# A fused two-layer graph kernel: new hand-written orders, one queue for half of layer 0's weights, TensorE transposes for the last batch

## The chip, the cores and the metric

The kernel runs on one core of a Trainium2 chip. A core has a matrix engine (TensorE, PE in the profile, with its weight loads listed apart as PEld), three engines that work on rows of 128 partitions (VectorE or DVE, ScalarE or ACT, GpSimd or POOL) and SyncE (SP), which here only issues DMAs. Each engine works through its own queue in order, and engines wait for one another by semaphores. The metric is the device time of one launch in microseconds.

## The reference

There are 64 batches of 256 tokens with 512 features and one weighted adjacency matrix per batch. Two layers follow each other, each with a residual and a layer norm:

```python
# layer 0
deg = jnp.sum(adj, axis=-1, keepdims=True)
agg = jnp.einsum('bij,bjf->bif', adj, x) / jnp.maximum(deg, EPS)
h   = relu(jnp.einsum('bnf,of->bno', jnp.concatenate([x, agg], axis=2), W))
x   = _layernorm(x + h)
# layer 1: 8 heads of 64
q, k, v = proj(Wq, bq), proj(Wk, bk), proj(Wv, bv)
scores = jnp.einsum('bhqd,bhkd->bhqk', q, k) * SCALE
attn = softmax(scores * (adj + adj)[:, None], axis=-1)
ctx = jnp.einsum('bhqk,bhkd->bhqd', attn, v)
x   = _layernorm(x + (jnp.einsum('bse,fe->bsf', ctx, Wo) + bo))
```

Everything is in float32.

## The kernel before, in words

**Steps and orders.** The kernel is a set of small steps, kept by name in a dictionary, and three texts that say in which order they are issued: START for the first batches, PLAN for one turn, which is run 28 times and takes two batches on, and END for the last batches. In START a word is name:batch, in PLAN name+n or name-n (batches counted from the turn's first), in END name:n with n counted back from 64, so that `:1` is the last batch, 63. Nothing reorders the steps afterwards: each engine gets its instructions in the order of the text. A step that uses a result waits for it by semaphore, and everything behind that instruction on the same engine waits as well.

**Products.** All large products are cut into 2 x 2 blocks and done with seven block products in place of eight (a Strassen-Winograd scheme). A letter names the product and a digit the block product: P (the first two batches) and L (later ones, by pairs of batches, cut twice; L546) are x times W of layer 0; Y is adj times the aggregate half (L709); Q makes q and k (L620); V and O are Wv and Wo (L493). The needed sums of blocks are steps of their own, mostly on POOL (xS, Ls, aS, bS, yS, cS; L432 and L567), for weights at the start (W0s, W0i, Wqs, Wvs, Wos). Results come out of PSUM by steps with k or j in the name: Yk and Yj on DVE (L731), Ok and Oj on DVE (L658, L474), Vk and Qk on ACT. Le takes L's results.

**Banks.** PSUM has eight banks, handed out in turn. A Y product group uses two. In the bank Ycb, the sums c (Y5, then Y3 on top) lie in the left half and b (Y2) in the right one: Y5, Yk5, Y3, Yj3 and Y2, Yj2 are the writers and readers of the two halves, and a product into one half waits for the readers of the other that stand before it in the order.

**Layer 0.** A batch's x is loaded twice: by Dx as rows, and by Dzx in blocks from which DVE makes the transposed xT0 and xT1 (L397). Dza and aT do this for adj, Dadj loads adj as rows, and deg is on DVE. After L (or P) and Y come relu and residual (AYr), statistics (AYb), factors on POOL (AYp, L671 to L673) and the norm on ACT (AYn, L677). The result is written to DRAM by Dway (L764) and read again by Dz1 (L770), turned by x1T (L777), and by Drest (L785) as the residual of layer 1, to which the step bo adds the output bias on POOL (L791). There is one buffer for rest.

**Layer 1.** The heads go in four pairs, a to d. For each: scores S (L812, eight products of 64 rows), m (mask and row maximum on DVE, L828), M (negation on POOL, L841), e and f (exponentials on ACT, L847), r (reciprocal of the sum, L859), n (the scaling on ACT, L864). The weights then have to be turned: T (32 x 32 blocks by DVE, L871), Dw (one DMA to DRAM, L876), Ds (four DMAs back, L884). C0a, C0b, C1a and C1b are the context products (L900), c0 and c1 copy them out (L916), O follows with the sums cS, then the norm (lb, lp, ln) and Dout (L939, four DMAs per batch).

**Weights.** They are loaded once in START by SP, except layer 0's W, which comes in two halves of its contraction, W0h0 and W0h1. Each half has two parts, part 0 for x and part 1 for the aggregate, each of four DMAs of 128 KB (L299, called from L301 to L305): part 1 is issued by ACT's queue, part 0 by SP's. The products of the first half's blocks are P1 and P5; from P2 on, the second half is used too. At most eight DMAs are in flight, since each takes one of eight semaphores. bv1 to bv3 fold bv times Wo into bo at the start.

The turn of PLAN has two places with contexts and scores (S, C). Around Y of the second batch it reads:

```
... Y6+3 Mb+1 Ok5+0 ed+1 O7+0 Yk6+3 aS4+3 Yj2+3 Ls51+4 Y3+3 ...
... V7+1 bS4+2 Dsa+0 V2+1 Vj7+1 xS1+4 Yj3+2 Y2+2 ...
```

Of the kernel before, what the change touches and what calls it, by code (L numbers as in the profile page):

```python
# [6 lines left out]

F32 = mybir.dt.float32
AF = mybir.ActivationFunctionType
# [3 lines left out]
P = 128  # L13
# [10 lines left out]
    Dzx:0 W0h0:0 Dzx:1 W0h1:0 xT0:0 xT1:0 Wv:0 xS3:0 xS1:0 P1:0 W0s1:0 xT0:1 P5:0 Dza:0 xT1:1 xS1:1 P1:1  # L24
    xS2:0 Wb:0 P5:1 Pk1:1 Pk1:0 Pk5:1 xS2:1 Dadj:1 Pk5:0 P2:0 W0s2:0 aT:0 Dadj:0 P6:0 W0i5:0 P6:1 W0s3:0
    Pk6:0 xS4:0 Dx:0 aS1:0 W0s4:0 aS3:0 P3:0 Wvs1:0 Pk6:1 Pj2:0 Dzx:2 P7:0 Pj3:0 deg:0 bS1:0 Y5:0 Pj7:0
    Y1:0 bS3:0 P4:0 Yk1:0 Dza:1 bS2:0 aS2:0 Pk4:0 Y6:0 Wq:0 Yk6:0 aS4:0 Yk5:0 xS3:1 Y7:0 xT0:2 Y3:0
    bS4:0 Y2:0 Yj3:0 Wvs2:0 Yj7:0 Yj2:0 Y4:0 AYr0:0 P7:1 xS4:1 AYb0:0 Yk4:0 AYp0:0 P2:1 AYr1:0 AYb1:0
    AYn0:0 xT1:2 P3:1 AYp1:0 Pj7:1 aT:1 AYn1:0 Dzx:3 Pj2:1 aS3:1 aS1:1 Pj3:1 deg:1 bS1:1 Dway:0 bS3:1
    Y5:1 Wo:0 Y1:1 Yk5:1 aS2:1 P4:1 W0i1:0 bS2:1 Yk1:1 Pk4:1 bv1:0 WqS:0 Y2:1 Y6:1 Dz1:0 xT0:3 Yk6:1  # L30
    Ls11:2 xT1:3 Y7:1 aS4:1 xS1:2 Wqs1:0 Y3:1 Dx:1 bv2:0 xS1:3 Yj7:1 Ls51:2 Ls52:2 bS4:1 L11:2 bv3:0
    L55:2 Dza:2 Le11:2 xS3:2 L15:2 Yj3:1 Y4:1 Ls12:2 Ls53:2 L16:2 Ls54:2 x1T:0 L51:2 L12:2 Le51:2 L52:2
    Le16:2 Yj2:1 yS1:0 L56:2 Yk4:1 Q1:0 Wqs2:0 Wvs3:0 AYr0:1 Ls13:2 Q5:0 Qk1:0 Wqs4:0 Le56:2 aT:2 V5:0
    AYr1:1 V1:0 yS2:0 AYb1:1 L17:2 Wvs4:0 Vk1:0 Q6:0 Wqs3:0 Ls14:2 yS3:0 W0i7:0 L57:2 Qk6:0 AYp1:1 V6:0
    AYb0:1 Qk5:0 Q7:0 yS4:0 W0i4:0 Vk6:0 AYp0:1 AYn1:1 V7:0 Le52:2 xS3:3 AYn0:1 Qj7:0 Q3:0 Le55:2 Dway:1
    Vk5:0 Le15:2 Drest:0 V3:0 Q4:0 Vj3:0 Le57:2 Le12:2 Qj3:0 L13:2 Le17:2 Vj7:0 L53:2 L14:2 Le53:2 L54:2
    Le13:2 Le14:2 V4:0 W0i6:0 Dz1:1 Le54:2 xS2:3 Qk4:0 Ls71:2 Sa:0 aS1:2 Vk4:0 W0i3:0 xS2:2 Sb:0 Dzx:5
    Ls61:2 Ls72:2 L61:2 ma:0 Ls63:2 V2:0 L2:2 mb:0 Ma:0 Dadj:2 Ls73:2 ea:0 Ls62:2 Wos1:0 L65:2 Lj2:2
    fa:0 L2:3 Le61:2 Ls64:2 Mb:0 Wos3:0 L66:2 eb:0 Q2:0 Le66:2 Lj2:3 fb:0 Vj2:0 Le65:2 L67:2 ra:0 na:0
    L63:2 Le67:2 L62:2 Qj2:0 L64:2 Le62:2 xS4:2 Sd:0 Le64:2 Le63:2 xS4:3 x1T:1 Sc:0 Ls31:2 L75:2 md:0  # L40
    yS1:1 Dzx:4 L72:2 L31:2 La12:2 L71:2 mc:0 L35:2 V5:1 Md:0 La12:3 ed:0 Q1:1 Le72:2 Dadj:3 Le31:2
    Ls32:2 Le75:2 Ls74:2 Le71:2 Ls33:2 L76:2 Mc:0 L36:2 aS3:2 Dx:2 Le76:2 ec:0 L73:2 Ls34:2 Le36:2 L41:2
    yS3:1 rb:0 Le35:2 fc:0 L77:2 deg:2 L37:2 Ls43:2 Q5:1 fd:0 Ls41:2 Le73:2 Le37:2 La22:2 Ta:0 nb:0 V1:1
    yS2:1 Le77:2 Dwa:0 Le41:2 L33:2 Qk1:1 Ls42:2 rc:0 L74:2 Le33:2 Ls44:2 L46:2 rd:0 Tb:0 bS3:2 nc:0
    L34:2 L32:2 bS1:2 Q6:1 Le32:2 Le74:2 Vk1:1 Le34:2 Qk5:1 La22:3 Tc:0 L45:2 nd:0 L42:2 Le45:2 Dwc:0
    Y5:2 Le46:2 V6:1 Dwb:0 Le42:2 Vk5:1 Dsa:0 L47:2 Vk6:1 yS4:1 L43:2 Qk6:1 Le47:2 Y1:2 bS2:2 Td:0 V3:1
    aS2:2 Wos2:0 Yk1:2 L44:2 Dwd:0 V7:1 Y6:2 Q3:1 Yk6:2 Dsb:0 Le43:2 xT0:5 bS4:2 xT0:4 Y2:2 Q7:1 xT1:5
    Dsc:0 Vj3:1 xS1:5 Vj7:1 Ls11:4 Y7:2 Qj7:1 Wos4:0 Q2:1 xT1:4 Yj7:2 bo:0 Yj2:2 Dsd:0 Y4:2 Yk5:2 Q4:1
    Yk4:2 AYr1:2 Qj2:1 Dza:3 aS4:2 V4:1 Qk4:1 Qj3:1 xS1:4 Le44:2 Y3:2 Ls53:4 Vk4:1 Yj3:2 Sa:1 AYb1:2
    C0a:0 AYr0:2 AYp1:2 C1a:0 AYb0:2 AYn1:2 ma:1 AYp0:2 C1b:0 C0b:0 xS3:5 AYn0:2 deg:3 Ls51:4 Sc:1 c0:0  # L50
    Dway:2 Ls12:4 aT:3 c1:0 Ls14:4 Sb:1 mc:1 aS1:3 bS1:3 Sd:1 mb:1 V2:1 Mc:1 bS3:3 ec:1 Y1:3 cS1:0 Y5:3
    md:1 fc:1 O2:0 bS2:3 O5:0 aS2:3 Yk1:3 Ma:1 Dx:3 aS3:3 L51:4 Ls13:4 Y6:3 Le51:4 Ls52:4 O1:0 ea:1
    Yk6:3 cS3:0 Y2:3 cS2:0 Dz1:2 Ok1:0 L56:4 Vj2:1 aS4:3 Y7:3 Yk5:3 Md:1 rc:1 L15:4 Yj2:3 bS4:3 nc:1
    L12:4 Yj7:3 Y3:3 Mb:1 Y4:3 O6:0 Yk4:3 fb:1 Yj3:3 L11:4 Oj2:0 cS4:0 L2:5 Ok6:0 Le11:4 Ok5:0 eb:1
    Ls54:4 AYr0:3 AYb0:3 fa:1 L16:4 L2:4 AYr1:3 AYp0:3 ed:1 AYb1:3 Le56:4 L55:4 Tc:1 AYn0:3 AYp1:3 O7:0
    fd:1 L52:4 Dwc:1 Oj7:0 L57:4 x1T:2 AYn1:3 Dza:4 O3:0 Le15:4 Le55:4 rb:1 rd:1 L13:4 yS1:2 Le16:4
    Le57:4 nd:1 L53:4 Le13:4 xS3:4 Dway:3 L17:4 O4:0 Le17:4 Ls73:4 ra:1 Oj3:0 L14:4 Td:1 L54:4 Q5:2
    Le54:4 xS2:5 nb:1 Ok4:0 Le12:4 xS2:4 Lj2:4 Ls61:4 lb0:0 V5:2 Le14:4 na:1 lb1:0 Q1:2 lp0:0 Dz1:3
    Lj2:5 Ls71:4 Ta:1 V1:2 Ls62:4 lp1:0 Q2:2 Vk1:2 Le53:4 Qk1:2 Dwa:1 Tb:1 yS2:2 ln1:0 yS3:2 L65:4 Dwb:1
    V6:2 Ls63:4 Dwd:1 Ls64:4 Dsc:1 L61:4 Vk6:2 Q6:2 Vk5:2 Le61:4 ln0:0 Qk5:2 L62:4 yS4:2 Qk6:2 V7:2 Q3:2  # L60
    Dsd:1 L66:4 Q7:2 Le66:4 Dsa:1 Vj7:2 Le65:4 Le62:4 Le52:4 V3:2 L67:4 Vj3:2 V2:2 Qj7:2 Le67:4 V4:2
    Qj3:2 Dsb:1 Vj2:2 L63:4 Qj2:2 Q4:2 Dout:0 L64:4 Qk4:2 Le64:4 Sa:2 Le63:4 Vk4:2 aT:4 La12:4 C1a:1
    x1T:3 Dx:4 C0a:1 xS4:4 xS4:5 ma:2 C0b:1 Ls31:4 yS1:3 C1b:1 Ls72:4 La12:5 Drest:1 c1:1 Sd:2 c0:1
    Dadj:4 Sb:2 md:2 Ls33:4 Ls32:4 Sc:2 Ls34:4 cS1:1 mb:2 L75:4 Md:2 L71:4 Ma:2 O2:1 mc:2 Mb:2 aS1:4
    L72:4 Dzx:7 fb:2 Ls74:4 L35:4 L32:4 aS3:4 Le71:4 ea:2 L31:4 Mc:2 Le35:4 L76:4 bo:1 Le31:4 O5:1 ec:2
    Dadj:5 deg:4 L33:4 eb:2 L36:4 Le75:4 Le76:4 L73:4 fa:2 Le36:4 cS2:1 L77:4 Le72:4 O1:1 Le73:4 Ls41:4
    ed:2 Ok5:1 Ls42:4 rb:2 Le32:4 L37:4 Ls44:4 Ok1:1 nb:2 Y1:4 cS3:1 Le33:4 O6:1 Le77:4 Le37:4 L74:4
    ra:2 cS4:1 Ok6:1 fc:2 V5:3 Tb:2 bS1:4 O7:1 fd:2 yS3:3 Yk1:4 Dwb:2 Oj2:1 O3:1 La22:4 Dzx:6 rc:2 Oj7:1
    nc:2 L34:4 Oj3:1 O4:1 Le74:4 rd:2 Le34:4 La22:5 Q5:3 na:2 Tc:2 Dwc:2 L41:4 nd:2 yS2:3 Y5:4 Le41:4
    Dsb:2 V1:3 Ls43:4 Ok4:1 lb0:1 bS2:4 L45:4 Vk1:3 aS2:4 L46:4 Ta:2 Qk5:3 lp0:1 Q1:3 Vk5:3 Td:2 Dwa:2  # L70
    V6:3 Qk1:3 Le46:4 Dwd:2 Le45:4 L42:4 Dsc:2 ln0:1 L47:4 Y6:4 Le47:4 Vk6:3 Q6:3 lb1:1 aS4:4 bS3:4
    Yk6:4 Y7:4 Dsa:2 Qk6:3 yS4:3 L43:4 V7:3 lp1:1 Le43:4 Le42:4 L44:4 Yk5:4 bS4:4 Q7:3 Yj7:4 ln1:1 xT0:7
    xT1:7 Dout:1 Y3:4 xS1:7 Qj7:3 Y2:4 bS3:5 Y4:4 Yj2:4 V3:3 Vj7:3 Dza:5 Yk4:4 Q4:3 Yj3:4 xT1:6 deg:5
    Q2:3 AYr1:4 Dsd:2 AYr0:4 Q3:3 AYb1:4 Drest:2 Le44:4 AYp1:4 xT0:6 V4:3 Vj3:3 AYb0:4 xS1:6 AYn1:4
    C0a:2 Ls11:6 Qj3:3 Qk4:3 AYp0:4 Qj2:3 C0b:2 Vk4:3 aT:5 C1a:2 AYn0:4 aS1:5 bS1:5 Dway:4 C1b:2 Ls53:6
    c1:2 Ls13:6 Sb:3 aS3:5 c0:2 Ls12:6 Sd:3 mb:3 bo:2 Sa:3 md:3 Sc:3 Y1:5 cS1:2 O2:2 ma:3 Dz1:4 Mb:3
    Y5:5 O5:2 bS2:5 Yk1:5 mc:3 Y2:5 aS2:5 Dx:5 O1:2 cS2:2 Ma:3 Y6:5 Ok5:2 cS3:2 V2:3 Ok1:2 bS4:5 Yk5:5
    Oj2:2 L11:6 aS4:5 Yj2:5 O6:2 Le11:6 Ls51:6 Yk6:5 fb:3 Ls14:6 Y7:5 Ok6:2 Md:3 Y3:5 cS4:2 Yj7:5 eb:3
    O7:2 Yj3:5 Ls52:6 x1T:4 fa:3 Y4:5 L51:6 O3:2 Yk4:5 ea:3 yS1:4 Oj7:2 Vj2:3 L2:7 Mc:3 Le51:6 Ls54:6
    AYr1:5 fd:3 AYb1:5 ed:3 L55:6 rb:3 L16:6 ra:3 AYp1:5 AYr0:5 O4:2 nb:3 AYb0:5 L52:6 xS3:7 Ok4:2 L56:6  # L80
    Oj3:2 AYp0:5 AYn1:5 L15:6 lb0:2 Q1:4 Le56:6 AYn0:5 Le15:6 L57:6 Dway:5 Le16:6 na:3 Dza:6 L17:6 Q5:4
    Le17:6 Tb:3 Le55:6 Qk1:4 L14:6 rd:3 Le57:6 Dwb:3 V5:4 Le52:6 ec:3 L53:6 Dadj:6 L54:6 Le14:6 Vk5:4
    L13:6 Lj2:7 Le54:6 xS2:7 L12:6 fc:3 Le53:6 L2:6 yS2:4 Le13:6 Qk5:4 xS2:6 rc:3 Ta:3 Ls61:6 nc:3 Q6:4
    lp0:2 lb1:2 Dwa:3 Dsb:3 Le12:6 lp1:2 Lj2:6 nd:3 V1:4 Tc:3 Q2:4 Ls62:6 yS3:4 Vk1:4 Td:3 Dwc:3 ln1:2
    Qk6:4 V6:4 Qj2:4 Dwd:3 L61:6 Dsa:3 Vk6:4 yS4:4 Q7:4 ln0:2 Le61:6 xS3:6 Ls63:6 Ls64:6 L65:6 Qj7:4
    Dout:2 Ls73:6 L62:6 L66:6 Le62:6 Q3:4 Le66:6 Le65:6 V3:4 Dsc:3 L67:6 Vj3:4 V7:4 L63:6 Dsd:3 Vj7:4
    Q4:4 deg:6 Le67:6 Qj3:4 V4:4 Qk4:4 L64:6 Vk4:4 Le64:6 xS4:7 Sb:4 Dz1:5 aT:6 xS4:6 Sc:4 Le63:6 Ls31:6
    La12:6 C0a:3 Drest:3 C0b:3 Ls71:6 aS1:6 C1a:3 Dzx:9 mb:4 Ls32:6 La12:7 C1b:3 mc:4 c1:3 Sd:4 Mb:4
    c0:3 Dx:6 Mc:4 Ls72:6
"""  # L90
PLAN = """
# [63 lines left out]
def kernel(  # L155
# [36 lines left out]
    nc = tc.nc  # L192
# [108 lines left out]
    def load_half(h):  # L301
        @step(f"W0h{h}")
        def _(_):
            load_weights(nc.scalar, w0_raw, 1, w0t[F:], slice(2 * h, 2 * h + 2))
            load_weights(nc.sync, w0_raw, 0, w0t[:F], slice(2 * h, 2 * h + 2))  # L305
# [692 lines left out]
```

## Time and profile before

| what | value |
|---|---|
| median of 3 runs | 3033.29 us (3032.24 to 3034.77) |
| the profiled execution | 3032.66 us |
| its span | 3030.7 us |
| instructions | 59847 |
| PE busy, granted clock over the span | 98%, 0.996 |
| DVE, POOL, ACT busy | 73%, 60%, 54% |
| DMA | 513.88 MB, 170 GB/s on average |

The profile is of one execution. It lists busy time by engine, the span in 40 slices, the groups of instructions by line with what they waited for, and the DMAs with the time from issue to landing. "Line" is the line of the kernel's source. Times of the order "start, duration" come from the trace of that execution; the mark in brackets behind an instruction is the idle time before it and what the trace took to be its releaser. Ends of matmuls are modelled, so their busy time overlaps, while their starts are recorded. DMAs issued show as SPq or ACTq, the queue of the engine that issues them.

Some durations that the parts below use: a 128 x 256 ACT exponential 0.50 us and its row sum, the DVE transpose T 1.23, Drest 6.0 from issue to landing, the writes wsa, wsb and wsc to DRAM 2.9 to 3.9.

### The profile page before, as it was taken

Reading aid. Unit: us, or ns where it says so; the run is one execution under the profiler, and the core shown is the slowest. Engines: PE = TensorE matmul, PEld = TensorE weight load, DVE = VectorE, ACT = ScalarE, POOL = GpSimd, SP = SyncE. Lnnn points to the kernel's source line nnn. Section 1 sums busy time; section 2 is a strip of 40 time slices with the busy share of each in tenths; the row PEclk is TensorE's granted clock in tenths of the full one; section 3 lists DMA queues with packets and bytes.
Section 4 is the critical chain, followed back from the end, with each engine's and each line's share of the span. In section 5 each row is a group of like instructions: output and inputs, shape, how many; then the busy total and the mean of one; then the engine's idle time right before and its main releaser. Section 6 shows DMA issues by size and latency. Waiting matters only on the chain.

```text
span 3030.7 us, 59847 instructions
## 1 busy us (share of the span) xinstructions
PE 2975.6 (98%) x18668; PEld 2530.5 (83%) x18668; DVE 2223.1 (73%) x6148; ACT 1628.6 (54%) x4995; POOL 1822.8 (60%) x3313
## 2 busy tenths in 40 slices
PE   7999999999999999999999999999999999999997
PEld 4888888888888888888888888888888888888885
DVE  6877777777777777777777777777777778777774
ACT  2556555455564555554555645655546556456565
POOL 4656656656566566566565666665665656656543
PEclk9999999999999999999999999999999999999998
DMA  7566675776766766657667566666676675676665
GB/s 160 135 190 176 158 186 155 179 184 158 178 166 155 188 173 162 182 154 181 177 163 182 160 161 182 173 166 179 155 183 180 159 185 156 167 181 171 161 178 146
DMA packets 494282, 513.88 MB, mean 170 GB/s; under 512 B 113936, under 2 KB 392464, under 8 KB 493968
## 3 DMA queue, kind: packets, MB, share of 16 engines
q1 hardware_dynamic: 493328, 509.02, 64.9%
q8 instruction: 151, 2.47, 0.4%
q10 hardware_dynamic: 640, 1.05, 0.2%
q14 instruction: 163, 1.34, 0.2%
HBM read 308.55 MB, written 201.33 MB: 168 GB/s over the span
## 4 chain that ended last, share of the span: by engine, by line
PE 94%; DVE 2%; POOL 1%; DMA 1%; issue 1%; SPq 0%; ACT 0%; DVEq 0%; POOLq 0%
PE Qa L620 15%; PE pc L900 7%; PE Qc L620 7%; PE Va L493 7%; PE Oa L493 6%; PE Qb L620 4%; PE Vc L493 4%; PE Oc L493 4%; PE Ya L709 4%; PE Ycb L709 3%; PE L L598 3%; PE scd L812 2%; PE scc L812 2%; PE sca L812 2%; PE scb L812 2%; PE Ob L493 2%
## 5 line engine op out<-in xcount | busy, mean ns | idle before, releaser
L636 ACT ACTIVATE qk<-Qa,bqk 128x128 f32<-128x128 f32 x768 | 218.9, 370 | 289.5 <-PE Qa L620 289.5
L677 ACT ACTIVATE x<-oy,mv 128x512 f32<-128x512 f32 x128 | 103.8, 811 | 337.8 <-POOL mv L673 319.3
L432 POOL TENSOR_TENSOR xS<-xT,xS 128x256 f32<-128x256 f32 x64 | 46.7, 732 | 267.3 <-PE L6a L546 182.9
L671 POOL TENSOR_SCALAR mv<-mv 128x1 f32<-128x1 f32 x256 | 70.2, 274 | 215.3 <-DVE mv L666 172.4
L916 ACT COPY cT<-pc 128x512 f32<-128x512 f32 x128 | 71.7, 587 | 224.2 <-PE pc L900 224.0
L847 ACT ACTIVATE sa<-sa,nmaxa 128x256 f32<-128x256 f32 x256 | 126.8, 498 | 107.9 <-POOL nmaxa L841 71.3
L432 POOL TENSOR_TENSOR yS<-yS,x1T 128x256 f32<-128x256 f32 x64 | 46.6, 728 | 214.0 <-PE Vc L493 208.3
L731 DVE SCALAR_TENSOR_TENSOR oy<-Ya,deg,oy 128x256 f32<-128x256 f32 x256 | 121.9, 476 | 65.0 <-PE Ya L709 61.9
L828 DVE CUSTOM_DVE_ANT_0 sd<-scd,adj 128x256 f32<-128x256 f32 x256 | 93.3, 421 | 98.1 <-PE scd L812 98.0
L847 ACT ACTIVATE sc<-sc,nmaxc 128x256 f32<-128x256 f32 x256 | 127.0, 501 | 64.2 <-POOL nmaxc L841 64.2
L791 POOL TENSOR_TENSOR rest<-rest,bo_sb 128x512 f32<-128x512 f32 x128 | 160.5, 1276 | 0.2 <-issue 0.2
L672 POOL TENSOR_TENSOR mv<-mv,neg_half 128x1 f32<-128x1 f32 x256 | 145.0, 567 | 21.3
L620 PEld LDWEIGHTS Qa<-yS,Wq 128*128 128x128 f32 x1024 | 124.2, 192 | 15.6 <-issue 13.4
L658 DVE TENSOR_TENSOR rest<-Oa,rest 128x256 f32<-128x256 f32 x192 | 81.0, 422 | 76.3 <-PE Oa L493 60.8
L636 ACT ACTIVATE qk<-Qc,bqk 128x128 f32<-128x128 f32 x256 | 73.5, 380 | 110.0 <-PE Qc L620 110.0
L828 DVE CUSTOM_DVE_ANT_0 sc<-scc,adj 128x256 f32<-128x256 f32 x256 | 93.2, 421 | 53.2 <-PE pc L900 53.2
L432 POOL TENSOR_TENSOR cS<-cT 128x256 f32<-128x256 f32 x128 | 93.6, 731 | 63.2 <-ACT cT L916 63.2
L847 ACT ACTIVATE sd<-sd,nmaxd 128x256 f32<-128x256 f32 x256 | 127.2, 501 | 5.8 <-POOL nmaxd L841 5.8
L847 ACT ACTIVATE sb<-sb,nmaxb 128x256 f32<-128x256 f32 x256 | 127.3, 501 | 3.9 <-POOL nmaxb L841 3.9
L432 POOL TENSOR_TENSOR yS<-x1T 128x256 f32<-128x256 f32 x128 | 94.2, 736 | 56.4 <-DVE x1T L777 54.9
L620 PEld LDWEIGHTS Qa<-yS,Wq_sums 128*128 128x128 f32 x1024 | 124.3, 192 | 3.7 <-issue 0.5
L620 PEld LDWEIGHTS Qa<-x1T,Wq 128*128 128x128 f32 x1024 | 124.4, 192 | 3.3
(289 smaller groups left out, 10047.4 us busy)
## 6 DMA issues: line engine op xcount, KB each, us to landing
zx<-in_x_dram SPq DMA_DIRECT2D x256, 128.0 KB, 3.7
x<-in_x_dram SPq DMA_DIRECT2D x256, 128.0 KB, 3.3
way<-x SPq DMA_DIRECT2D x64, 512.0 KB, 3.2
z<-way SPq DMA_DIRECT2D x256, 128.0 KB, 4.0
rest<-way SPq DMA_DIRECT2D x64, 512.0 KB, 6.0
wsa<-sa SPq DMA_DIRECT2D x64, 512.0 KB, 3.9
wsc<-sc SPq DMA_DIRECT2D x64, 512.0 KB, 2.9
wsb<-sb SPq DMA_DIRECT2D x64, 512.0 KB, 3.5
```

Of the source, the lines that this page charges most:

```text
L432: steps[f"{s}{k}"] = lambda b: engine.tensor_tensor(place(b, k == 3), left(b), right(b), op)
L493: nc.tensor.matmul(ps[:, :width].rearrange("p (m o) -> p m o", o=G), lhsT=left(k, b, c), rhs=w(OUTER[k])[:, :, c], start=first and c == 0, ...
L620: nc.tensor.matmul(ps.rearrange("p (m j q) -> p m j q", m=2, j=2)[:, m, j], lhsT=wqk(OUTER[k])[:, m, c, j * P : (j + 1) * P], rhs=left_y(k ...
L636: nc.scalar.activation(part_q(b, t, n)[:, m, j], ps.rearrange("p (m j q) -> p m j q", m=2, j=2)[:, m, j], AF.Identity, bias=bqk[:, m, c : ...
L672: nc.gpsimd.tensor_tensor(mv[:, 1:2], mv[:, 1:2], neg_half, ALU.pow)
L709: nc.tensor.matmul(ps[:, G:] if acc == "b" else ps[:, :G], lhsT=left(b), rhs=right(b), start=k in (5, 1), stop=True, skip_group_check=True,)
L731: nc.vector.scalar_tensor_tensor(h, ps[:, G:] if acc == "b" else ps[:, :G], held["deg", b][:, t : t + 1], h, ALU.mult, ALU.add)
L791: nc.gpsimd.tensor_tensor(rest, rest, bo_sb, ALU.add)
L812: nc.tensor.matmul(sc(b, j)[:, t], lhsT=qk[d, 0, hp, t * P : (t + 1) * P], rhs=qk[d, 1, hp].rearrange("d (t b m) -> d b t m", t=NT, m=L), ...
L828: nc.vector.tensor_tensor_reduce(out=s[:, :, :, r], in0=sc(b, j)[:, t].rearrange("p (a c l) -> p a c l", a=A, l=L), in1=held["adj", b][:, ...
L847: nc.scalar.activation(rows(b)[:, r], rows(b)[:, r], AF.Exp, bias=of("nmax", b)[:, r : r + 1], accum_out=of("total", b)[:, r : r + 1],)
L900: nc.tensor.matmul(ps[j * D : (j + 1) * D, hp % 2], lhsT=held["v", b][:, c, h * D : (h + 1) * D], rhs=held[f"s{name}", b][:, :, c, j * NT ...
```

## The change

Three things change.

1. All three order texts are replaced. The steps are the same ones, apart from point 3. In the new PLAN, Y3 and Y2 of the two batches stand so, and the contexts and scores of one place are grouped (four contexts, then four scores):

```diff
-... Y6+3 Mb+1 Ok5+0 ed+1 O7+0 Yk6+3 aS4+3 Yj2+3 Ls51+4 Y3+3 ...
+... Y6+3 Dza+4 L15+4 Yk6+3 aS4+3 O7+0 cS4+0 rc+1 Ok5+0 nc+1 Yj2+3 Y3+3 ...
-... Y5+3 Dx+3 mc+1 O1+0 Ma+1 cS3+0 fa+1 Y1+3 O5+0 Ok1+0 Dz1+2 mb+1 Y2+3 ...
+... Y5+3 O1+0 aS2+3 Dz1+2 cS2+0 Y1+3 Ok1+0 L51+4 Ls12+4 Yk5+3 Y2+3 ...
-... Drest+1 L63+4 Vk4+2 L64+4 ... Mc+2 c0+1 Mb+2
+... La12+4 C0a+1 c1+1 C0b+1 xS4+4 Ls31+4 Drest+1 c0+1
```

The last pair of lines is the end of the turn; the bias step of the same batch, bo-1 in the next turn, is its 20th word before and its 27th after.

START begins with batch 1 in place of batch 0, and Wo is loaded where Wv was:

```diff
-    Dzx:0 W0h0:0 Dzx:1 W0h1:0 xT0:0 xT1:0 Wv:0 xS3:0 xS1:0 P1:0 W0s1:0 xT0:1 P5:0 Dza:0 xT1:1 xS1:1 P1:1
+    Dzx:1 W0h0:0 Dzx:0 W0h1:0 xT0:1 xT1:1 xS1:1 W0s1:0 P1:1 Dza:0 xT0:0 xT1:0 P5:1 Pk1:1 xS1:0 Wo:0
```

In END, the last batch's scores come as "V4:1 Qj3:1 Q4:1 Vk4:1 Dsd:2 Qk4:1 Sb:1 Sa:1 ...", where before Q4, V3, V4 and V2 of that batch came after its first scores, "Sa:1".

2. Part 1 of W0h1 goes to SP's queue:

```diff
-            load_weights(nc.scalar, w0_raw, 1, w0t[F:], slice(2 * h, 2 * h + 2))
+            load_weights(nc.sync if h else nc.scalar, w0_raw, 1, w0t[F:], slice(2 * h, 2 * h + 2))
```

3. For the last batch, T, Dw and Ds of all four head pairs are gone. n writes its rows to a new tile sn, which takes the place of layer 0 buffers, and the turning is done by TensorE against an identity that POOL makes (step id: a memset and a select), into a PSUM bank, from which ACT (c = 0) and DVE (c = 1) copy to the layout that C reads:

```diff
+            if last(b):
+                size, tag = ((2 * NT * F, "oy0"), (NT * F, "xT0"), (NT * F, "xT1"), (NT * F, "xS"))[hp]
+                tile_of(f"sn{name}", b, [P, size], tag=tag)
...
+        def by_tensor(c):
+            @step(f"X{name}{c}")
+            def _(b):
+                ps = bank(f"X{name}{c}", b)
+                for r in range(R):
+                    k = r * N + c * P
+                    nc.tensor.transpose(ps[:, r * P : (r + 1) * P], of("sn", b)[:, k : k + P], held["ident", b][:, :P])
+
+            @step(f"XC{name}{c}")
+            def _(b):
+                dst = of("s", b)[:, :, c].rearrange("k b r m -> k r b m")
+                src = held[f"X{name}{c}", b].rearrange("k (r b m) -> k r b m", r=R, m=L)
+                if c == 0:
+                    nc.scalar.copy(dst, src)
+                else:
+                    nc.vector.tensor_copy(dst, src)
```

That is 32 TensorE transposes of 128 x 128, four copies on ACT and four on DVE, in place of four DVE transposes, four DMAs out and sixteen DMAs back. In END they come as "Xc1 Xc0 ... Xa0 ... XCc1 ... Xb0 Xb1 XCa0 Xd0 XCb0 Xa1 XCd0 Xd1 XCa1 XCc0 XCb1 Drest C1a XCd1 C0a C0b C1b" of batch 63.

## The prediction

> **What bounds the kernel now.** I read the page's head and clock row first, then busy time by stretches, then the waits of TensorE, then its instructions in order of time around those waits.
>
> ```profile
> span 3030.7 us, 59847 instructions
> PE 2975.6 (98%) x18668; PEld 2530.5 (83%) x18668; DVE 2223.1 (73%) x6148; ACT 1628.6 (54%) x4995; POOL 1822.8 (60%) x3313
> PEclk9999999999999999999999999999999999999998
> ```
>
> The profiled execution took 3032.66 us, 1.96 of them outside its span; the median is 0.63 above it. TensorE (PE) is the bound, at full clock. But its busy time is modelled, so 98% doesn't say what is to be had. I went by the distance from matmul to matmul instead. Back to back a 512-column product takes 0.429 us, a 256-column one 0.216, a 128-column one 0.112 (below: sixteen of Q start 1.78 apart), a score or context matmul 0.108. Priced so, the kernel's products come to 2907.2 us. So 123.5 us are recoverable at most: 33.5 up to 275.0 us (12.8 of them before the first product), 58.7 in the 28 turns (92.76 each, for 90.66 of products: 2.10), 22.2 in the last stretch, and 9.0 behind the last product.
>
> ```profile
> core 0: us, PE busy (x) PEld busy (x) DVE busy (x) ACT busy (x) POOL busy (x), PEclk, DMA share, GB/s
> 0.00:100.00 100.00, 76.33 (x334) 51.16 (x335) 67.87 (x141) 25.17 (x64) 51.83 (x82) 1.00 0.68 148
> 1500.00:2000.00 500.00, 498.12 (x3155) 426.67 (x3154) 370.82 (x1039) 268.99 (x829) 306.58 (x562) 1.00 0.66 170
> 3000.00:3030.70 30.70, 12.59 (x52) 8.75 (x52) 4.52 (x11) 2.80 (x4) 7.36 (x12) 0.67 0.37 98
> ```
>
> The idle time lies at the two ends, and at the end the granted clock is 0.67.
>
> ```profile
> PE Pa L576 <- DMA W<-in_w0t_dram: 12.8, 1, 12.8
> PE pc L900 <- DMA sb<-wsb: 7.9, 1, 7.9
> PE Ycb L709 <- POOL xs L567: 5.5, 28, 0.2
> PE pc L900 <- DMA sa<-wsa: 2.8, 1, 2.8
> ```
>
> Three waits to look at: layer 0's weights at the start, the last batch's attention weights on their way through DRAM, and one that recurs in each of the 28 turns. The last is named after POOL, but the order of time shows another releaser:
>
> ```profile
> 1997.40 1.03 PE L493 MATMUL Oa<-Wo,cS 128*128 128x256 f32 x4
> 1997.60 0.48 DVE L731 SCALAR_TENSOR_TENSOR oy<-Ya,deg,oy 128x256 f32<-128x256 f32 x1
> 1998.00 0.47 DVE L731 SCALAR_TENSOR_TENSOR oy<-Ycb,deg,oy 128x256 f32<-128x256 f32 x1
> 1998.63 0.67 PE L709 MATMUL Ycb<-oy,aS 128*128 128x256 f32 x2 [0.20 <-POOL xs L567]
> ```
>
> Y3 writes one half of the bank Ycb; Yj2 on DVE (1998.00 to 1998.47) reads the other, behind Yk6 (1997.60). The four O7 products (0.86) end their slots at 1998.26, Y3 starts at 1998.63: 0.37 here, 0.44 averaged over the turns. Y2 waits likewise, for Yj3 behind Vj7: 0.38. The rest of a turn's 2.10 us is 1.29 of changes between full, score and context products.
>
> **The turn: -5.6 us (range -9 to 0).** No work is added or taken away; products stay 90.66. I walked the new order.
> - Changes: before, one of the two places goes context, scores, full (0.55), the other scores, context, scores, full (0.75), 1.29. After, both are all contexts, all scores, full: 2 x 0.55 = 1.09. Gain 0.20.
> - Y3+3 now has L15+4 and O7 between Y6 and itself, 0.43 + 0.86 = 1.30. In that time DVE does Yk6 0.39, rc 0.09, Ok5 0.34, Yj2 0.48, in its order; with 0.2 from product to DVE and 0.15 back that is 1.6 to 1.7. It stays about 0.4 late. Queued behind Y3 on PE is everything.
> - Y2+3 has Y1 and L51, 0.43 + 0.43, after O1, but waits for Yk5 behind Ok1 on DVE: 1.1 against 0.86. With the allowance by which the same sum falls short of before's two waits (0.15), 0.38 late. The turn's other products keep 0.15 us or more, and the loads of turned weights (Ds) are issued 4.7 us earlier than the contexts need them, 6.75 before.
> So the waits stay: 0.20 x 28 = 5.6. At worst a margin of 0.15 fails and takes that back; at best one of the waits shrinks by 0.1.
>
> **The start: -5.0 us (range -8 to +1).** The first four of zx, 128 KB each, have landed at 8.2 us; transfers of 128 KB land one per 0.62. Before, part 0 of the first half of W0 (SP's queue) landed at 9.6 to 12.7, interleaved with part 1 of the second half (ACT's queue), which nobody needs before 18 us. After, that second half is behind the first on SP; ACT's queue holds four. The first half is complete near 10.7, so P1:1 starts 2.1 us earlier. P2's weights, the second half, still land near 18.2 (the total is unchanged), and the four DMAs moved stand ahead of za, Wo and adj on SP; at 1.0 us of issuing each (4.12 for four of W0 before) that alone delays these by some 4. From there it is my walk: P7 (1.46 of waiting before), the two Y waits of 1.1 and that of 2.2 lose their causes, since batches are interleaved the other way round; the p_bv wait for Wo (1.97) goes, since Wo takes Wv's early place among the loads. I get Q's first product at 53 to 54.4 against an equal point at 60.4, 6 to 7.4 gained. Against it: Wv comes late (near 58.8; V5 waits 0.9) and DVE is 90% busy from 60 to 100 us. I take 5.0. Below zero: if the transfers of Wq, way and Wv push z1 back by 7, all is lost again; one more us is what the late Wv could cost.
>
> **The end: -2.4 us (range -7 to +2).**
>
> ```profile
> 2975.19 1.13 PE L812 MATMUL sca<-qk 64*128 64x256 f32 x8
> 3006.85 1.98 PE L900 MATMUL pc<-sb,v 128*64 128x256 f32 x8 [7.90 <-DMA sb<-wsb]
> 3008.58 1.86 PE L900 MATMUL pc<-sc,v 128*64 128x256 f32 x8
> 3010.27 1.05 PE L900 MATMUL pc<-sd,v 128*64 128x256 f32 x8
> ```
>
> The last batch's first scores start at 2975.19, the span ends 55.5 later. ACT ends nd at 2997.2; then comes DVE's transpose (1.23), the write to DRAM, the load, and pc starts at 3006.85 at half clock. After, the order puts four more products of Q and V before the first scores (1.78 + 3 x 0.86 = 4.4). From those scores on: ACT has sixteen exponentials (0.49 each), four n (1.6 each), copies and a layer norm in a row and ends nd 22.9 later; Xd (8 x 0.11), its copies from PSUM and the two last contexts take 5.9; c1 0.6, cS1 0.75, bo 2.5, cS2 0.73, the O products, norm and output as now, 17.9 at full clock (19.6 before, partly at 0.67). Sum 46.7, against 55.5 less 4.4: -4.4. Removed are 4 transposes on DVE and 20 DMAs; the 8 copies hang on ACT (behind nd) and DVE, which idles then. The two make_identity instructions on POOL run while POOL is idle.
>
> Clock. A transpose is a 128-column product; the nearest row is Q's:
>
> ```profile
> 63.69 1.95 PE L620 MATMUL Qa<-x1T,Wq 128*128 128x128 f32 x16
> 65.47 1.95 PE L620 MATMUL Qc<-yS,Wq_sums 128*128 128x128 f32 x16
> ```
>
> By it 32 transposes take 3.6 us. The Trainium skill ("TensorE: Matmul & The Clock Gate", Part 4: PE-mode transpose) speaks against the change: about 275 ns each in a kernel, and they don't count as work for the clock. By the page the 32 take 8.8, and 24 of them lie in PE's idle time; d's eight add 1.3. If the clock falls to half before d's contexts, these and the O products behind pay what before paid: (1.70 - 0.86) a context, up to 4 in all. I take 2 of these 4 away from 4.4. At best (-7) ACT's row is 2.5 shorter, at worst everything is at half clock and the copies out of PSUM, whose target lies in pieces of 32, cost double.
>
> **Sum.** 5.6 + 5.0 + 2.4 = 13.0; 3032.66 - 13.0 = 3019.7 for an execution like the profiled one, 3020.3 by the median. I give 3020.
>
> **The rivals.**
> 1. *The turn's two waits vanish.* For: they are the only waits that recur, and the change moves what stands before them. Against: the walk above finds both still 0.3 to 0.4 short. Both gone: 28 x 0.82 = 23 more, 2997; one gone: 3009. Chance 0.13.
> 2. *The start's gain is given back and the end stays cold.* For: bytes are unchanged, the DMA share is 0.68 in the first 100 us; at 100 us it is DVE's queue that leads. Against: P1 demonstrably waits for W0. 3020.3 + 5.0 + 2.4 = 3027.7: no change. Chance 0.13.
> 3. *Slower, by one mechanism: rest comes late in the turn.*
>
> ```profile
> rest<-way SPq DMA_DIRECT2D x64, 512.0 KB, 6.0
> ```
>
> Drest+1 now stands 6.0 us of PE's work before bo-1 (10.8 before), where the row's median is 6.0 us and the slowest 9.2. If rest is late, POOL stands at bo, with Ls34 (slack 1.0 to L34) and cS2 (2.3 to O6) queued behind it; PE then waits at L34. With 0.4 of margin before POOL, it costs from a landing of 7.4 us on, and the whole gain from 13/28 = 0.46 more: about 7.9 in every turn. If the typical landing under the new order is 8.5, 28 x 1.1 = 31 against 13 gained: about 3051. Against: only one in ten lands over 7.7 now, and those would cost some 0.3. Chance 0.08.
>
> The likeliest case holds 0.66, from 3012 to 3027. The range reaches over most of the first two rivals: 3003 to 3029. What can be told from no change is 0.2%, 6.1 us, so faster is below 3027.2: 0.66 and the first rival's 0.13, less a little for the upper end: 0.78. Same: 0.15. Slower, above 3039.4: 0.07.
>
> **What would show it.** In the profile after: 92.55 us per turn, with Ycb still waiting some 0.4 twice (wrong if the waits on L709 shrink or L34 appears among them); the first product near 10.8 and Q's first near 54; no wait for sb<-wsb, nd to the last pc some 6 us, the transposes 0.11 or 0.28 apart and PEclk between 0.5 and 1 in the last 30 us; rest landing in about 6 us with bo not waiting. If bo waits for DMA in most turns, the third rival has it.

## The result, and the profile after

The changed kernel takes 3019.61 us (median of 5 runs, 3019.02 to 3021.61) against 3033.29 for the kernel before: a ratio of 0.9957, with a 95% interval from 0.9943 to 0.9972. Its profiled execution is one of 3019.61 us, with a span of 3017.7, 13.0 us less than before. The head and the clock row of its page:

```profile
span 3017.7 us, 59666 instructions
...
PE 2972.0 (98%) x18700; PEld 2541.1 (84%) x18700; DVE 2219.4 (74%) x6148; ACT 1638.0 (54%) x4999; POOL 1818.5 (60%) x3315
...
PEclk9999999999999999999999999999999999999999
```

The shares of busy time are within a point of those before, so they can't show what changed. What does is the trace, cut at the first product of the first turn and at the first one of END. Products are priced as in the prediction, and stalls are the rest of a stretch:

| stretch | before | after | products before, after | stalls before, after |
|---|---|---|---|---|
| up to the first turn | 275.2 | 268.3 | 241.6, 239.0 | 33.6, 29.3 |
| the 28 turns | 2597.3 | 2593.1 | 2538.6, 2538.6 | 58.7, 54.5 |
| END and what follows | 158.2 | 156.3 | 127.0, 133.2 | 31.2, 23.1 |

The new START holds 2.6 us of products less and END as much more, and 3.6 us of END are the transposes. So the stretches gained 4.3, 4.2 and (8.1 less 3.6) 4.5 us. The first of these is the least certain, since one execution is compared with one: in the six profiled executions with the old START the first turn began at 273.8 to 278.8 us, half of them below 275, and in the three with the new START and queue at 268.3 to 268.5. The waits of TensorE after, longest first:

```profile
PE Pa L576 <- DMA zx<-in_x_dram: 10.9, 1, 10.9
PE Ycb L709 <- DVE oy L731: 8.1, 29, 1.4
PE Ycb L709 <- POOL nmaxb L846: 4.5, 28, 0.2
PE Ya L709 <- DVE oy L731: 2.6, 3, 1.0
PE Xb L905 <- ACT snb L876: 2.2, 1, 2.2
```

The first product starts 1.9 us earlier, no context waits for a load from DRAM (the longest such wait was 7.9), and two waits still recur 28 times, both at Ycb. The second is named after POOL, as before; which engine it is comes next.

**The turn after.** PE and DVE in order of time around Y2+3, then around Y3+3:

```profile
1987.04 0.59 PE L709 MATMUL Ya<-oy,aT 128*128 128x256 f32 x2
...
1987.41 0.42 DVE L658 TENSOR_TENSOR rest<-Oa,rest 128x256 f32<-128x256 f32 x1 [1.25 <-PE Oa L493]
...
1987.47 0.59 PE L546 MATMUL L5a<-W_sums,xS 128*128 128x256 f32 x2
...
1987.75 0.47 DVE L731 SCALAR_TENSOR_TENSOR oy<-Ycb,deg,oy 128x256 f32<-128x256 f32 x1
...
1988.28 0.48 PE L709 MATMUL Ycb<-oy,aT 128*128 128x256 f32 x1 [0.21 <-DVE oy L731]
```

```profile
1990.98 1.03 PE L493 MATMUL Oa<-Wo,cS 128*128 128x256 f32 x4
...
1991.15 0.17 DVE L864 RECIPROCAL totalc<-totalc 128x4 f32<-128x4 f32 x1
...
1991.23 0.39 DVE L658 TENSOR_TENSOR rest<-Oc,rest 128x256 f32<-128x256 f32 x1
...
1991.54 0.48 DVE L731 SCALAR_TENSOR_TENSOR oy<-Ycb,deg,oy 128x256 f32<-128x256 f32 x1
...
1992.16 0.45 PE L709 MATMUL Ycb<-oy,aS 128*128 128x256 f32 x1 [0.16 <-POOL nmaxb L846]
```

In both, the last DVE line before the product is the reader of the other half of Ycb, and ahead of it stand DVE instructions that don't concern it: Ok1 (1987.41), rc and Ok5 (1991.15, 1991.23). The product starts 0.06 to 0.14 us after the reader's end. The slots of the products ahead end at 1987.90 (0.43 behind the start of L5) and at 1991.84 (0.86 behind that of O7); from there to the product's start is the wait, 0.38 and 0.32. Another 0.10 and 0.08 are lost between the two matmuls of Y2 and of Y3, so the two cost 0.48 and 0.40.

**The end after.** PE from the last batch's first scores on, then ACT's nd (the last scaling), and the granted clock around the transposes (columns: stretch, length, PE busy with its instructions, PEclk, DMA share, GB/s):

```profile
2971.29 1.13 PE L817 MATMUL scb<-qk 64*128 64x256 f32 x8
...
2991.56 2.52 PE L905 MATMUL Xb<-ident,snb 128*128 128x128 f32 x8 [2.16 <-ACT snb L876]
2993.88 1.06 PE L905 MATMUL Xd<-ident,snd 128*128 128x128 f32 x4
...
2998.91 1.03 PE L934 MATMUL pc<-sd,v 128*64 128x256 f32 x8
```

```profile
2992.61 1.69 ACT L876 ACTIVATE snd<-sd,totald 128x256 f32<-128x256 f32 x4
```

```profile
2991.50:2993.00 1.50, 1.44 (x4) 0.50 0.93 247
2993.00:2994.50 1.50, 1.50 (x8) 0.50 0.09 25
2994.50:2996.00 1.50, 1.33 (x11) 0.89 0.65 218
2996.00:3010.00 14.00, 10.49 (x60) 1.00 0.04 15
```

From the first scores to the span's end it is 46.4 us now. As long as there are products, the clock is at half for some 3.3 us only, and all contexts run at full clock.

### The profile page after: what moved, and what is told of

Read it like the earlier page. It is cut to its first block, busy times and chain, and to the rows that moved or that the text cites. A ratio compares the mean times of both kernels' runs of the same rounds, so it can differ in the third digit from the quotient of the medians.

```text
span 3017.7 us, 59666 instructions
## 1 busy us (share of the span) xinstructions
PE 2972.0 (98%) x18700; PEld 2541.1 (84%) x18700; DVE 2219.4 (74%) x6148; ACT 1638.0 (54%) x4999; POOL 1818.5 (60%) x3315
## 4 chain that ended last, share of the span: by engine, by line
PE 91%; DMA 3%; DVE 3%; POOL 2%; issue 1%; SPq 0%; ACT 0%; DVEq 0%; ACTq 0%; POOLq 0%
PE Qa L620 15%; PE pc L934 8%; PE Qc L620 8%; PE Va L493 7%; PE Oa L493 6%; PE Qb L620 4%; PE Vc L493 4%; PE L L598 4%; PE Ya L709 3%; PE Oc L493 3%; PE Ycb L709 3%; PE scd L817 2%; DMA z<-way 2%; PE L6a L546 2%; PE L4a L546 2%; PE L3a L546 2%
## 5 line engine op out<-in xcount | busy, mean ns | idle before, releaser
L852 ACT ACTIVATE sc<-sc,nmaxc 128x256 f32<-128x256 f32 x256 | 127.0, 498 | 157.7 <-POOL nmaxc L846 147.0
L649 ACT COPY v<-Va 128x256 f32<-128x256 f32 x192 | 73.0, 380 | 240.0 <-PE Va L493 240.0
L833 DVE CUSTOM_DVE_ANT_0 sa<-sca,adj 128x256 f32<-128x256 f32 x256 | 93.2, 421 | 110.2 <-PE sca L817 99.4
L876 ACT ACTIVATE sc<-sc,totalc 128x256 f32<-128x256 f32 x252 | 107.5, 497 | 96.0 <-DVE totalc L864 96.0
L671 POOL TENSOR_SCALAR mv<-mv 128x1 f32<-128x1 f32 x256 | 58.4, 228 | 158.6 <-DVE mv L666 145.0
L567 POOL TENSOR_TENSOR xs<-xS 128x128 f32<-128x128 f32 x248 | 122.6, 509 | 23.0 <-PE L1a L546 22.8
L611 POOL TENSOR_TENSOR oy<-oy 128x512 f32<-128x512 f32 x62 | 77.9, 1274 | 93.6 <-DVE oy L559 93.4
L876 ACT ACTIVATE sd<-sd,totald 128x256 f32<-128x256 f32 x252 | 107.7, 508 | 45.7 <-DVE totald L864 45.6
L731 DVE SCALAR_TENSOR_TENSOR oy<-Ycb,deg,oy 128x256 f32<-128x256 f32 x192 | 91.4, 477 | 52.9 <-PE Ycb L709 52.7
```

What stands on the lines that cost most here:

```text
L731: nc.vector.scalar_tensor_tensor(h, ps[:, G:] if acc == "b" else ps[:, :G], held["deg", b][:, t : t + 1], h, ALU.mult, ALU.add)
L833: nc.vector.tensor_tensor_reduce(out=s[:, :, :, r], in0=sc(b, j)[:, t].rearrange("p (a c l) -> p a c l", a=A, l=L), in1=held["adj", b][:, ...
L852: nc.scalar.activation(rows(b)[:, r], rows(b)[:, r], AF.Exp, bias=of("nmax", b)[:, r : r + 1], accum_out=of("total", b)[:, r : r + 1],)
L876: nc.scalar.activation(dst, src, AF.Identity, scale=of("total", b)[:, r : r + 1])
```

## The experiments

The kernel before was timed again beside each of these, with medians of 3031.5 to 3032.0 us; so ratios to it are given, and spans of profiled executions are compared.

**1. The two waits of the turn taken away.**

```diff
-Y1+3 Ok1+0 L51+4 Ls12+4 Yk5+3 Y2+3
+Y1+3 Yk5+3 Ok1+0 L51+4 Ls12+4 Y2+3
-Yk6+3 aS4+3 O7+0 cS4+0 rc+1 Ok5+0 nc+1 Yj2+3 Y3+3
+Yj2+3 Yk6+3 aS4+3 O7+0 cS4+0 rc+1 Ok5+0 nc+1 Y3+3
```

> The changed kernel with three words of PLAN moved: Yj2+3 ahead of Yk6+3, and Yk5+3 ahead of Ok1+0, so that the two TensorE products that still wait in each turn (Y3+3 0.40 us, Y2+3 0.48) find their DVE readers served earlier. Nothing else is changed. Theory (the two waits are DVE queueing ahead of the readers of the shared bank Ycb, and nothing else is within 0.15 us of them): both vanish, 28 x 0.88 = 24.6 us less than the changed kernel, about 2995 us, turn near 91.75 us. Rival (another wait takes their place: O6 behind the later Ok1, Y7 behind the later Yk6, L47 or L2): half or less of it, 3007 to 3019. Rival (the two waits are not of that cause, but of the semaphore round trip itself): no change, 3019.

Measured: 2994.9 us, 0.9879 of before (0.9863 to 0.9896); span 2993.3, 24.4 less than the changed kernel. Its waits of TensorE have no row with a count of 28:

```profile
PE Pa L575 <- DMA zx<-in_x_dram: 10.9, 1, 10.9
PE Ya L708 <- DVE oy L730: 2.6, 3, 1.0
PE Xb L904 <- ACT snb L875: 2.2, 1, 2.2
PE Ycb L708 <- DVE oy L730: 1.4, 1, 1.4
```

The theory held: a turn takes 91.70 us (91.75 expected), so both waits come from DVE's queue, also the one that the page puts down to POOL, and nothing takes their place. The turns alone gained 25.4 us; the end was 0.8 longer in this execution, with the same END. Two words of an order text, moved, are worth more than the whole change. Whether a bank of its own for each half would do the same wasn't tried.

**2. The same in the kernel before.**

```diff
-Yk6+3 aS4+3 Yj2+3 Ls51+4 Y3+3
+Yj2+3 Yk6+3 aS4+3 Ls51+4 Y3+3
-Vj7+1 xS1+4 Yj3+2 Y2+2
+Yj3+2 Vj7+1 xS1+4 Y2+2
```

> The kernel before with two words of PLAN moved and nothing else: Yj2+3 ahead of Yk6+3, and Yj3+2 ahead of Vj7+1, so that on DVE the readers of the bank Ycb come ahead of the other work there. Theory (both recurring waits, 0.436 and 0.381 us, are DVE queueing): 28 x 0.8 = 22.5 us faster than before, about 0.9926 of it, turn near 91.96. Rival (in this order the margins behind the two are too small, O6, O7 and V6 have 0.1 us or less): half of it, 10 to 15 us. Rival (queueing on DVE is not the cause): no change.

Measured: 3009.31 us, 0.9917 (0.9903 to 0.9932), a turn of 91.95. As expected (91.96), and no other wait grew by more than 0.01 us a turn.

**3. Contexts and scores grouped, in the kernel before.** In PLAN, Sc+2 and Sb+2 are moved behind C1b+1, with mc+2, mb+2 and Mc+2 behind them.

> The kernel before with only the scores Sc+2 and Sb+2 of PLAN moved behind the four contexts of their place (and mc, mb, Mc with them), so that both places of a turn read contexts, scores, full products, as in the changed kernel. Theory (of the 0.149 us per turn between the two kernels, 0.20 is the saved change between kinds of product, and 0.05 is lost again in the two waits): turn 92.76 - 0.20 = 92.56, 28 x 0.20 = 5.6 us faster than before. Rival (the new order's gain comes from other waits and the grouping is worth nothing): no change. Rival on the other side (contexts come 1.9 us earlier and wait for their loaded weights): slower, with waits at L900 in many turns.

Measured: 3043.95 us, 1.0035 (1.0023 to 1.0047). The changes between kinds of product fell from 1.29 to 1.09 us per turn, as expected. But a new wait of 0.63 at O5-1 stands in 27 of the 28 turns, which neither the theory nor a rival had named. PE's waits, then POOL in order of time:

```profile
PE Oc L493 <- POOL cS L432: 10.1, 28, 0.4
```

```profile
2045.41 0.23 POOL L841 TENSOR_SCALAR nmaxb<-nmaxb 128x4 f32<-128x4 f32 x1 [1.14 <-DVE nmaxb L828]
2045.60 0.73 POOL L432 TENSOR_TENSOR cS<-cT 128x256 f32<-128x256 f32 x1
2046.79 0.22 POOL L841 TENSOR_SCALAR nmaxd<-nmaxd 128x4 f32<-128x4 f32 x1 [0.46 <-DVE nmaxd L828]
2046.98 0.73 POOL L432 TENSOR_TENSOR cS<-cT 128x256 f32<-128x256 f32 x1
```

The later scores make POOL stand at Mb+2 and Md+0 (1.14 and 0.46, for DVE's maxima), and the sum cS1-1 for O5 is queued behind (2046.98).

**4. The same, with that sum first.** cS1-1 moved ahead of cS3-1, nothing else.

> As before_grouped, with one word more: cS1-1 ahead of cS3-1 in PLAN, so that on POOL the sum that O5-1 waits for no longer stands behind cS3-1 and Md+0. before_grouped was slower than before because O5-1 then waited 0.63 us in every turn, while the changes between kinds of product fell by 0.20 us. Theory (the 0.63 is queueing on POOL and the 0.20 is the grouping's own worth): the wait goes, turn near 92.56, 5 to 6 us faster than before. Rival (cS1-1 itself comes too late since Mb+2 waits for DVE ahead of it): a wait of 0.2 to 0.6 stays, between 0 and 10 us slower than before.

Measured: 3031.0 us, 0.9996 (0.9987 to 1.0006), a turn of 92.75. The wait at O5 is gone and the 0.20 us remain saved, but O6 and L73 now wait some 0.1 each and take nearly all of it back. Neither the theory nor the rival named that. So the grouping is shown to save 0.20 us of changes per turn; whether that remains as a net gain depends on the order around it, and here it didn't.

**5. The queue alone undone.** Part 1 of W0h1 back on ACT's queue, orders as changed.

> The changed kernel with only the queue undone: part 1 of W0h1 on ACT's queue again, order texts as changed. Theory (the second half of W0 on a second queue takes transfer time from the first half): the first product starts at 12.5 to 13 instead of 10.93, 1.6 to 2.0 us slower, about 3021.4. Rival (the gain at the start is that of the loads' order alone, batch 1 first and Wo early): no change, within 0.5 of 3019.6, first product near 11. Rival on the other side (SP relieved of four DMAs, 2 us of its issuing, lets za, Wo and adj go earlier): 1 to 2 us faster.

Measured: 3022.12 us, 0.9969 (0.9958 to 0.9980), span 3020.0, 2.3 more than the changed kernel; the first product at 13.25 instead of 10.93, the first turn 2.4 later. The theory's side, with 2.3 for 1.6 to 2.0.

```profile
PE Pa L576 <- DMA zx<-in_x_dram: 13.3, 1, 13.3
```

The trace says why. The last load of part 0 of the first half lands at 13.12 us here and at 10.58 in the changed kernel. In both, loads land one by one, about 0.62 apart, and here four loads of ACT's queue land in between (8.96 to 12.47): 4 x 0.62 = 2.5.

**6. The last batch through DRAM, in the new order.** T, Dw and Ds put back for batch 63, X, XC and id taken out; n writes in place.

> The changed kernel with only the last batch's turning undone: DVE transposes, writes to DRAM and loads back for batch 63, in the new order (no TensorE transposes, no copies out of PSUM, no identity). Theory (the bounce through DRAM is what the contexts wait for, some 9 us from nd to the last loaded piece against 3 us for the TensorE way, and the first two contexts then run at half clock): 5.5 to 7.5 us slower than the changed kernel, about 3026, with a wait of some 8 us at a context product. Rival (the gain at the end comes from the order of scores and products, the transposes only repay their own 3.6 us): 0 to 2 us slower.

Measured: 3034.06 us, 1.0004 (0.9998 to 1.0011), span 3031.9: 14.2 more than the changed kernel, twice the expected.

```profile
2987.30 1.13 PE L491 MATMUL Oa<-Wo_sums,cT 128*128 128x256 f32 x4 [2.03 <-DVE rest L472]
2994.22 1.97 PE L932 MATMUL pc<-sa,v 128*64 128x256 f32 x8 [5.79 <-DMA sa<-wsa]
3000.06 1.97 PE L932 MATMUL pc<-sc,v 128*64 128x256 f32 x8 [3.86 <-DMA sc<-wsc]
3008.30 1.98 PE L932 MATMUL pc<-sb,v 128*64 128x256 f32 x8 [6.27 <-DMA sb<-wsb]
3010.86 1.97 PE L932 MATMUL pc<-sd,v 128*64 128x256 f32 x8 [0.58 <-DMA sd<-wsd]
```

```profile
2997.27 1.70 ACT L874 ACTIVATE sd<-sd,totald 128x256 f32<-128x256 f32 x4 [1.43 <-DVE totald L862]
```

The last contexts start 12.0 us later than in the changed kernel (3010.86 for 2998.91). Some 7 of it are the way through DRAM, as expected. But ACT also starts nd 4.7 later (2997.27 for 2992.61), for which no expectation allowed: the transposes on DVE (1.25 each) stand ahead of rc, of rd and of batch 62's O parts. How much of these 4.7 another placing of the T steps would save wasn't tried, so the 14.2 are not the price of the way through DRAM alone. And every context runs at half clock (1.97 for 1.03).

**7. Only the TensorE transposes, in the old order.** The kernel before, with 32 transposes and 8 copies for T, Dw and Ds of batch 63.

> The kernel before, with its own three orders and queues, and only the last batch turned by TensorE (32 transposes, 8 copies; these put behind O4 and the n steps; T, Dw, Ds of batch 63 left out). Theory (before, ACT ends nd at 2997.2, 33.5 us before the span's end; in the changed kernel the same stretch takes 23.5): 9 to 10 us faster than before, about 3023.5, which is twice the 4.5 us by which the changed kernel's end is shorter, since the new END also puts 4.4 us of products ahead of the last batch's scores. Rival (the end gained 4.5 us by the transposes and nothing was lost by the order): 4 to 5 us faster than before, about 3028.5.

Measured: 3028.9 us, 0.9991 (0.9983 to 1.0000), span 3026.9: 2.6 us less by the medians, less than the theory and than the rival had it. PE behind the contexts, then POOL:

```profile
2999.99 1.03 PE L935 MATMUL pc<-sd,v 128*64 128x256 f32 x8
...
3002.79 1.03 PE L494 MATMUL Oc<-Wo_sums,cS 128*128 128x256 f32 x4
3010.60 2.08 PE L494 MATMUL Oa<-Wo_sums,cS 128*128 128x256 f32 x4 [6.79 <-POOL cS L433]
```

```profile
3001.74 0.72 POOL L433 TENSOR_TENSOR cS<-cT 128x256 f32<-128x256 f32 x1 [4.43 <-ACT cT L951]
3007.38 2.48 POOL L792 TENSOR_TENSOR rest<-rest,bo_sb 128x512 f32<-128x512 f32 x2 [4.91 <-DMA rest<-way]
```

The contexts were done at 3001, 10 us earlier than before, just as the theory had it. The gain went into a new wait: POOL stands at bo for the residual, because there is one buffer rest, batch 62's output leaves it only at 3000 to 3002, and so the load goes out at 3003.6. cS2, which O6 needs, is behind bo. Meanwhile TensorE has next to nothing to do, and the last O products run at half clock (2.08 for 1.13):

```profile
3003.00:3010.00 7.00, 0.81 (x4) 0.94 0.24 76
3010.00:3018.00 8.00, 6.79 (x15) 0.50 0.00 1
```

**8. The same, with the residual in a buffer of its own.**

```diff
+        if last(b):
+            rest = held["rest", b] = tile_of("rest_last", b, [P, 2 * NT, F], tag="oy1")[:, :NT]
+        else:
+            rest = tile_of("rest", b, [P, NT, F])
...
-Drest:2 ea:1 ... Ok6:2 cS4:2 ... Dout:2 Drest:1 C0a:1
+Drest:2 Drest:1 ea:1 ... Ok6:2 cS4:2 bo:1 ... Dout:2 C0a:1
```

> As tensor_turn_in_old_order, with one more thing: the last batch's residual gets a buffer of its own (that of its layer 0 result, free by then) in place of the one buffer rest, so its load is issued some 20 us earlier and the bias step bo is done before the contexts. Theory (there the contexts were done at 3001.0, 10 us earlier than before, and then O6 waited 6.8 us for POOL, which waited for rest, whose buffer was free only after the output of batch 62 had left): that wait goes, and the half clock behind it; 10 to 12 us faster than before. Rival (the wait is POOL's sums cS and not rest): 4 us faster than before, as without it.

Measured: 3021.03 us, 0.9958 (0.9943 to 0.9972), 11.0 less by the medians. In the profiled execution the end is 12.1 us shorter than before (146.1 for 158.2), while its first turn began 1.5 later. The wait at O6 fell from 6.8 to 0.9:

```profile
PE Oa L494 <- POOL cS L433: 0.9, 1, 0.9
```

This settles it: before, the end was behind DRAM; with TensorE's transposes in the old order it is behind the one buffer. The new order ends batch 62 earlier (its output goes out from 2990.2 on, the residual load for batch 63 at 2993.7), so POOL doesn't stand at bo there, and O6 waits 1.1. The old orders and queues with these two steps at the end are thus as fast as the whole change (0.9958 and 0.9957).

**9. All of it together.** Experiment 1, the residual apart, a new end of ACT's, DVE's and TensorE's work for the last batch, and W0i5 later in START.

> The changed kernel with the two waits of the turn moved away as in waits_moved, and a new end: the last batch's residual in a buffer of its own, ACT's work for the last batch in one row (the layer norm of batch 62 behind it), TensorE transposes and contexts of pairs a, b, c ahead of those of d, and all copies out of PSUM but d's first on DVE. In START, W0i5 on DVE is moved behind AYb1:0. Theory (the end hangs on ACT's row and then on POOL, the start's Y2:0 on DVE behind W0i5): end 6 us shorter and start 1.0 to 1.5 shorter than in waits_moved, about 2987. Rival (the end is bound by the chain behind the contexts, from c1 to the output, which stays): 1 to 3 us, 2992 to 2994.

Measured: 2990.32 us, 0.9858 (0.9841 to 0.9874). In the profiled executions the start is 1.3 us shorter than in experiment 1, as expected, but only 0.5 in experiment 10, which has the same START. The end is 4.0 shorter (expected 6): between the theory and its rival.

**10. A second end.** Batch 62's norm behind the last batch's copies and sums; O2, O5, O1 for O2, O1, O5.

> As combined, with the end in another order once more: batch 62's norm (lb, lp, ln) behind the last batch's copies and sums, and O2, O5, O1 instead of O2, O1, O5, so that cS2, which overwrites what O5 reads, may start earlier. Theory (in combined, C1a waited 1.1 us for a copy behind batch 62's statistics on DVE, and cS2 waited 2.25 us for O5): 1.8 to 2.8 us less than combined, near 2988. Rival (the end hangs on ACT's row alone, the rest has slack): no change.

Measured: 2988.93 us, 0.9853 (0.9837 to 0.9869). The end is 0.9 us shorter than in 9, the wait at C1a 0.5 instead of 1.1. Half of the least that was expected; the fastest kernel here, but not told apart from 9 by its interval.

## Why the prediction was right, point by point

The time (3020 for 3019.61) and the sum (13.0 for 13.0 of span) were met. But that they were met so closely is luck. For the turn, the start and the end 5.6, 5.0 and 2.4 were predicted and 4.2, 4.3 and 4.5 measured, and the errors (1.4 and 0.7 too much, 2.1 too little) cancel.

- *The turn*: right in kind. "So the waits stay" is what the trace shows: Y3 0.40 and Y2 0.48 where 0.4 and 0.38 were given, and the changes between kinds of product at 1.09. The mis-sized term is Y2: the sum counted the wait before its first matmul (0.38) and left out a pause of 0.10 between its two. Y3 and a small pause at O6 gave 0.04 each that was not counted. So most turns take 92.58, a gain of 0.18. In two of 92.9 Y2 waits 0.35 longer (why wasn't looked at), which makes 0.15 on average, 4.2 us in all. Experiment 1 then shows the cause of both waits, which the prediction had only walked.
- *The start*: the first product came at 10.93 for 10.8, and experiment 5 shows the queue to be worth 2.3. The delay of some 4 us that was given for the loads behind on SP was too much: eight loads of W0 went out in 4.40 us, 0.55 each and not 1.0. P7's wait and that for Wo are gone, as said. The step that failed is "the two Y waits of 1.1 and that of 2.2 lose their causes": there are seven waits of 1.0 to 1.5 us at Y products now, 8.3 in all where 7.2 were. They are for DVE and POOL, so the order of batches only changed which of their work stands in front. Along with these pauses the granted clock fell, which no part of the working had (stretch, length, PE busy, PEclk, DMA share, GB/s):

```profile
48.00:50.00 2.00, 1.07 (x3) 0.79 1.16 208
50.00:56.00 6.00, 5.33 (x13) 0.50 1.15 220
56.00:62.00 6.00, 6.00 (x45) 1.00 0.95 211
```

  At p_bv alone that cost 1.35 us: its sixteen products took 4.80 us, for 3.45 at full clock. Q's first product starts at 58.05, not 54. What made up for it came behind: TensorE's stalls from 60 us to the first turn fell from 6.7 to 4.6, where a worse DVE queue had been feared.
- *The end*: the walk was right to 0.3 us: 46.4 for 46.7 from the first scores, nd 22.9 after them as given, 5.6 for 5.9 from nd to the last context, 17.9 behind. The mis-sized term is the clock, for which 2 of 4 us were taken off: it fell to half for 3.3 us only, in which TensorE mostly had to wait for ACT's n anyway, and next to nothing of the 4 was paid. For the transposes the row of Q was the right guide: they stand 0.11 us apart at full clock. The 8.8 us set against it came from a misread figure (last section).
- *The first rival* was refuted for the change (both waits are there) and confirmed as a price: 24.4 us when they are really moved away. What spoke against it in the walk, "both still 0.3 to 0.4 short", is what the trace shows.
- *The second rival* was right that the start would give something back (the Y waits), but 4.3 us of gain remained there, and the end did not stay cold.
- *The third rival* lost its ground: its row of rest is quicker under the new order.

```profile
rest<-way SPq DMA_DIRECT2D x64, 512.0 KB, 4.8
```

  It was 6.0 before, so the margin of 6.0 us was enough, and POOL never stood at bo; the slowest load took 6.1 us, where it was 9.2. Why rest lands faster wasn't tried: the loads around its new place in SP's queue are others.

## What to carry to other kernels

In this program a product that shares a PSUM bank waits for the readers of the other half: look at what stands ahead of these readers in the queue of the engine that reads, and put the reader first. Here that was worth 0.8 to 0.9 us in a turn of 92.8, in either order, or 23 to 25 us in 28 turns, where the whole change gave 13. A faster way to turn the last operand gains only what the next resource allows, here the single buffer of the residual: when a wait is taken away, name what the engine behind it needs next and when its buffer comes free. Of a predicted sum, check the terms and not only the total.

## What the runs showed of the hardware

In these runs transposes on TensorE kept its clock up and even brought it back. In experiment 7 thirty-two of them, 0.109 us apart (eight from 2993.42 to 2994.29) but for one pause of 0.4, ran at a granted clock of 1.00:

```profile
2993.40:2995.40 2.00, 2.00 (x20) 1.00 0.00 0
2995.40:2997.30 1.90, 1.83 (x16) 1.00 0.00 0
```

In the changed kernel the twenty behind the wait of 2.16 us started at 0.50 and stood 0.21 apart where ACT didn't hold them up, and the clock was back at 1.00 some 3.3 us later, with nothing but transposes in between. The Trainium skill ("TensorE: Matmul & The Clock Gate", Part 4: PE-mode transpose) says that transposes don't count as work for the clock; these traces don't agree. They list them as MATMUL with the identity, and don't show whether the mode that the page speaks of was on.

The page's 275 ns is another matter. It is the length of one transpose and not the distance to the next, and as a length it agrees with the trace (behind the colon: shortest, median and longest in ns, then the first and the last start):

```profile
L905 PE MATMUL Xc<-ident,snc x8: 272/300/330, 2987.0 to 2988.7; 128*128 128x128 f32 x8
```

At full clock one is 0.27 us long by the modelled end, as a 128-column product of Q is, while the next starts 0.11 behind its start where ACT doesn't hold it up. The prediction multiplied the length by 32.

In the changed kernel's start short pauses went with half clock. From 43 us on, products of 0.4 to 0.9 us at a time stood between pauses of 1.0 to 1.3 us; the granted clock was 0.79 between 48 and 50 us and 0.50 between 50 and 56, and 1.00 again behind a stretch with hardly a pause. The kernel before kept 1.00 there, with fewer but longer pauses: 2.4, 0.8, 0.7 and 2.1 us ahead of products between 47 and 57 us. No run here varied the pauses by themselves, so how many of them it takes stays open.
